# A feature map in SBUF with the batches of a chain innermost, in a kernel of row and column scans

## The chip, the cores and the metric

The kernel runs on one NeuronCore of a Trainium2 chip. The metric is the device time of one execution in microseconds (us); for several executions it is the median. The profile and the trace come from one further execution, taken by the hardware profiler. TensorE (PE) does the matrix products and reads its moving operand from SBUF; VectorE (DVE), ScalarE (ACT) and GpSimd (POOL) do the rest; SyncE (SP) issues the transfers between HBM and SBUF.

## The reference

Two layers follow each other, each `x + scan(groupnorm(x))`. The input is float32, 32 batches of 48 channels, 64 rows and 128 columns. A scan runs over the map four times, and each pass goes step by step: down over the rows, up, right over the columns, left. A step adds to a row (or column) the five-tap convolution of the one before it, taken along the row (or column), over all 48 channels:

```python
def step(w, b):
    def f(carry, inp):
        nxt = inp + _conv1d(carry, w, b)      # 48 x 48 channels, 5 taps, padding 2
        return (nxt, nxt)
    return f
...
x = x + scan0(_gn(x)); x = x + scan1(_gn(x))  # _gn: 16 groups of 3 channels
```

Down and up share their weights. The 32 batches are independent of each other; within one, each step needs the result of the step before it.

## The kernel before

**Tiling.** Channels of even positions along the convolved axis sit on partitions 0 to 47, those of odd positions on 64 to 111, so one step is three accumulated matrix products of 112 x 112 (lines 173, 174 and 177 of `step`): with the pair of positions itself, the pair before and the pair after. In float32 each product is two matmul instructions in the trace, so a step is six. The moving operand of a step has the pairs of positions of four batches: 4 x 64 columns in the down and up passes, 4 x 32 in the right and left passes; the second and third product leave out one pair at the edge (4 x 63 and 4 x 31).

**The map.** Four batches (G = 4) make a chain, and the map of a chain is one tile `[112, G, 64, 2, 32]`: batch, pair of columns, r, pair of rows. It is 64 KB on each partition. `row(h)` (line 195) is every 64th element of it, one element at a time: 256 elements, 256 bytes apart within a batch. `col(v)` (line 198) is four runs of 32 adjacent elements, one for each batch.

**The step.** After its products a VectorE instruction on line 180 adds the PSUM tile, the bias and `inp` (a row or column of the map) and writes `dst`. In the down pass `inp` and `dst` are the same row of the map, and the next step's moving operand is that row; the last row of the pass goes to the tile `last`, which is contiguous. In the up pass `dst` and the moving operand are `carry` tiles, contiguous, and `place` (line 188) copies each carry with two ScalarE instructions of 48 partitions into the map, where the right and left passes read it. In those passes `inp`, `dst` and the moving operand are columns of the map.

**Two lanes.** Two chains, one for each lane, are in flight in turn: while VectorE finishes a step of one lane, PE runs the six matmuls of the other. "Round" below means one step of both lanes, 12 matmuls. There are eight chains, so four pairs of them one after the other, each with two layers: eight times down, up, right and left.

**Boundaries.** Between two layers of a pair (and between two pairs) each batch goes through `add_scan` (line 106, POOL: adds the map of the batch to its x tile of 112 x 4096), the store, where the next chain starts the load of its x, the statistics of the group norm (lines 119 to 145, mostly VectorE) and `normalize`: two ScalarE instructions (line 152, partitions 0 to 47) and two POOL instructions (line 159, partitions 64 to 111), each of 48 x 2048, which read x with a step of 128 elements and write runs of the map. The first down step needs all four batches of its chain. The order of the instructions on each engine is set by the tile framework when the program is built; each engine runs its own in that order.

Of the kernel before, what the change touches and what calls it, by code (L numbers as in the profile page):

```python
"""Two pre-activation layers x + scan(groupnorm(x)), each scan running down, up, right and
left over the feature map with a 5-tap convolution across the other axis per step.

Layout. Channels of even and odd positions along the convolved axis sit side by side on the
partitions (even at 0..47, odd at 64..111, zeros between), so that one convolution step is
three accumulated 112 x 112 matrix products: with the pair before, the pair itself and the
pair after. The map of a batch lies in SBUF as [pair of w][r][pair of h]:
  down/up:     partition side = parity of w, r = parity of h
  right/left:  partition side = parity of h, r = parity of w
The scans run in place; the up scan writes its rows to where the second layout has them.  # L10

Batches go in chains of G, and two chains are in flight step by step in turn, so that what
a step of one chain waits for runs under the other's matrix products.
"""
# [7 lines left out]
F32 = mybir.dt.float32  # L22
# [5 lines left out]
P = ODD + C  # L28
# [11 lines left out]
def kernel(  # L40
# [34 lines left out]
        cpool.tile([P, G, WP, 2, HP], F32, tag=f"map{i}", name=f"map{i}")  # L75
# [3 lines left out]
        cpool.tile([P, G, WP], F32, tag=f"last{i}", name=f"last{i}") for i in range(LANES)  # L79
# [3 lines left out]
    # The partitions between the two sides carry zeros throughout.  # L83
# [10 lines left out]
    def load_x(lane: int, src: bass.AP, b: int) -> bass.AP:  # L94
        """Batch j of a chain always goes to tile j % NX of its lane."""
# [9 lines left out]
    def add_scan(lane: int, j: int, xt: bass.AP):  # L105
        nc.gpsimd.tensor_tensor(  # L106
            xt, xt, maps[lane][:, j].rearrange("c p r q -> c q (p r)"), ALU.add
        )

    def stats(xt: bass.AP, key: str):  # L110
        """Per-partition scale and offset of the group norm of one batch."""
# [21 lines left out]
        # 1 / sqrt(var), with a Newton step behind the table's square root.  # L133
# [14 lines left out]
    def normalize(lane: int, j: int, xt: bass.AP, scale: bass.AP, offset: bass.AP):  # L148
        view = xt.rearrange("c q (p r) -> c p r q", r=2)
        for hs in range(2):  # L150
            hsl = SIDES[hs]
            nc.scalar.activation(  # L152
                maps[lane][SIDES[0], j, :, hs, :],
# [6 lines left out]
                maps[lane][SIDES[1], j, :, hs, :],  # L160
# [7 lines left out]
    def step(lane: int, layer: int, way: int, key: str, prev, inp, dst):  # L168
        """dst = inp + conv(prev) + bias over [P, G, pairs]."""
# [20 lines left out]
    def scan(lane: int, layer: int, key: str, early):  # L190
# [3 lines left out]
        def row(h):  # L194
            return m[:, :, :, h % 2, h // 2]
# [119 lines left out]
```

## Time and profile before

| | |
|---|---|
| Median of the 3 timed runs | 8442.6 us |
| Lowest and highest | 8436.63 and 8445.32 us |
| Span of the profiled execution | 8440.7 us |
| PE busy | 6745.4 us, 80% |
| VectorE busy | 3721.4 us, 44% |
| ScalarE busy | 1902.0 us, 23% |
| GpSimd busy | 1264.6 us, 15% |
| DMA queue of the loads and stores | 20.7% of the 16 engines |

The span runs from the first to the last instruction of the profiled execution. Busy shares are means over stages that differ: in the passes PE is busy nearly throughout, at the boundaries hardly at all. [...] The timeline gives start and duration of instructions; those that follow each other with the same form are merged, with their count.

### The profile page before, as it was taken

How to read it: one execution, taken by the hardware profiler on the slowest of the kernel's cores; microseconds unless marked ns; L12 is line 12 of the kernel's file. 1: busy time of each engine (PE TensorE's matmuls, PEld its weight loads, DVE VectorE, ACT ScalarE, POOL GpSimd, SP SyncE). 2: the span in 40 equal slices, each digit the busy share in tenths (PEclk: the TensorE clock that was granted, in tenths of full speed). 3: DMA queues.
4: the chain of work that ended last, by engine and by line, in shares of the span. 5: the costliest groups of instructions: out<-in, count | busy, mean ns of one | idle time of the engine just before them, and what ended most of it. 6: DMA issues, size and time to landing. Idle time of an engine off the chain costs nothing. (4 is left out here: it accounts for less than half of the span.)

```text
span 8440.7 us, 85243 instructions
## 1 busy us (share of the span) xinstructions
PE 6745.4 (80%) x36736; PEld 5026.5 (60%) x36736; DVE 3721.4 (44%) x7235; ACT 1902.0 (23%) x2241; POOL 1264.6 (15%) x199
## 2 busy tenths in 40 slices
PE   4999559994499955999449995599944999559993
PEld 2479524894247952489424795248942479524893
DVE  5345533553334553355333455335532345533552
ACT  3070110700207011070020701107012070110700
POOL 4000330003300033000330003300043000330004
PEclk9999779997699977999769997799976999779997
DMA  9000240005700024000570002400057000340005
GB/s 94 0 1 1 44 76 0 1 1 74 105 0 1 1 41 79 0 1 1 75 105 0 1 1 46 74 0 1 1 75 105 0 1 1 46 74 0 1 1 90
DMA packets 497403, 258.09 MB, mean 31 GB/s; under 512 B 5392, under 2 KB 496912, under 8 KB 497024
## 3 DMA queue, kind: packets, MB, share of 16 engines
q1 hardware_dynamic: 496640, 251.68, 20.7%
q8 instruction: 287, 4.70, 0.2%
q10 hardware_dynamic: 384, 0.96, 0.0%
q14 instruction: 92, 0.75, 0.0%
HBM read 151.95 MB, written 100.66 MB: 30 GB/s over the span
## 5 line engine op out<-in xcount | busy, mean ns | idle before, releaser
L106 POOL TENSOR_TENSOR x<-x,map 112x4096 f32<-112x4096 f32 x64 | 694.3, 10866 | 6611.4 <-issue 3290.5
L123 PE MATMUL ps_stat_x<-mv_x,mask_sb 112*112 112x1 f32 x64 | 16.4, 326 | 728.1 <-DVE mv_x L121 722.2
L188 ACT COPY map<-last 48x256 f32<-48x256 f32 x32 | 21.9, 683 | 2469.5 <-DVE last L180 2469.2
L123 PEld LDWEIGHTS ps_stat_x<-mv_x,mask_sb 112*112 112x112 f32 x64 | 14.9, 286 | 731.8 <-DVE mv_x L121 724.8
L135 ACT ACTIVATE std_m<-var_m 112x1 f32<-112x1 f32 x32 | 6.5, 203 | 1850.4 <-DVE var_m L132 1850.3
L123 PE MATMUL ps_stat_m<-mv_m,mask_sb 112*112 112x1 f32 x64 | 16.4, 326 | 473.8 <-DVE mv_m L121 448.6
L119 DVE BATCH_NORM_STATS2 st_x<-x 112x6 f32<-112x512 f32 x256 | 155.6, 679 | 513.9 <-DMA x<-in_x 513.7
L135 ACT ACTIVATE std_x<-var_x 112x1 f32<-112x1 f32 x32 | 6.5, 203 | 1615.1 <-DVE var_x L132 1615.1
L159 POOL TENSOR_SCALAR map<-x,scale_x,offset_x 48x2048 f32<-48x2048 f32 x64 | 277.8, 4341 | 346.3 <-DVE offset_x L145 340.3
L119 DVE BATCH_NORM_STATS2 st_m<-x 112x6 f32<-112x512 f32 x256 | 160.5, 679 | 340.7 <-POOL x L106 340.7
L159 POOL TENSOR_SCALAR map<-x,scale_m,offset_m 48x2048 f32<-48x2048 f32 x64 | 271.6, 4244 | 195.4 <-DVE offset_m L145 171.3
L123 PEld LDWEIGHTS ps_stat_m<-mv_m,mask_sb 112*112 112x112 f32 x64 | 14.9, 286 | 477.7 <-DVE mv_m L121 450.7
L152 ACT ACTIVATE map<-x,offset_x,scale_x 48x2048 f32<-48x2048 f32 x64 | 279.3, 4364 | 44.9 <-DVE offset_x L145 41.3
L152 ACT ACTIVATE map<-x,offset_m,scale_m 48x2048 f32<-48x2048 f32 x64 | 273.1, 4268 | 51.6 <-DVE offset_m L145 34.1
L130 PE MATMUL ps_stat_m<-sq_m,mask_sb 112*112 112x1 f32 x64 | 16.5, 328 | 151.9 <-DVE sq_m L129 151.9
L180 DVE SCALAR_TENSOR_TENSOR map<-ps_1L1d,b_sb,map 112x256 f32<-112x256 f32 x62 | 75.3, 1215 | 123.7 <-PE ps_1L1d L177 117.9
L180 DVE SCALAR_TENSOR_TENSOR map<-ps_3L1d,b_sb,map 112x256 f32<-112x256 f32 x62 | 75.5, 1217 | 123.1 <-PE ps_3L1d L177 118.0
L180 DVE SCALAR_TENSOR_TENSOR map<-ps_7L0d,b_sb,map 112x256 f32<-112x256 f32 x62 | 76.3, 1231 | 121.2 <-PE ps_7L0d L177 115.6
L180 DVE SCALAR_TENSOR_TENSOR map<-ps_7L1d,b_sb,map 112x256 f32<-112x256 f32 x62 | 75.5, 1217 | 123.0 <-PE ps_7L1d L177 117.9
L180 DVE SCALAR_TENSOR_TENSOR map<-ps_5L1d,b_sb,map 112x256 f32<-112x256 f32 x62 | 75.4, 1216 | 123.0 <-PE ps_5L1d L177 117.9
L180 DVE SCALAR_TENSOR_TENSOR map<-ps_3L0d,b_sb,map 112x256 f32<-112x256 f32 x62 | 76.4, 1232 | 120.7 <-PE ps_3L0d L177 115.4
L180 DVE SCALAR_TENSOR_TENSOR map<-ps_5L0d,b_sb,map 112x256 f32<-112x256 f32 x62 | 76.3, 1231 | 120.6 <-PE ps_5L0d L177 115.5
(617 smaller groups left out, 19622.9 us busy)
## 6 DMA issues: line engine op xcount, KB each, us to landing
x<-in_x SPq DMA_DIRECT2D x128, 768.0 KB, 16.3
mid<-x SPq DMA_DIRECT2D x64, 768.0 KB, 12.1
x<-mid SPq DMA_DIRECT2D x64, 768.0 KB, 16.0
out<-x SPq DMA_DIRECT2D x64, 768.0 KB, 12.6
w_sb<-in_w ACTq DMA_DIRECT2D x1, 882.0 KB, 12.2
mask_sb<-in_mask ACTq DMA_DIRECT2D x1, 49.0 KB, 1.9
b_sb<-in_b ACTq DMA_DIRECT2D x1, 2.6 KB, 5.4
```

What stands on the lines that cost most here:

```text
L106: nc.gpsimd.tensor_tensor(xt, xt, maps[lane][:, j].rearrange("c p r q -> c q (p r)"), ALU.add)
L119: nc.vector.bn_stats(st[:, s, :], flat[:, bass.ts(s, SEG)])
L123: nc.tensor.matmul(ps[:, 0:1], mask_sb, mv[:, 0:1], start=True, stop=True)
L130: nc.tensor.matmul(ps[:, 1:2], mask_sb, sq, start=True, stop=True)
L135: nc.scalar.activation(std, var, AF.Sqrt)
L152: nc.scalar.activation(maps[lane][SIDES[0], j, :, hs, :], view[hsl, :, 0, :], AF.Identity, bias=offset[hsl], scale=scale[hsl],)
L159: nc.gpsimd.tensor_scalar(maps[lane][SIDES[1], j, :, hs, :], view[hsl, :, 1, :], scale[hsl], offset[hsl], ALU.mult, ALU.add,)
L180: nc.vector.scalar_tensor_tensor(dst, ps, b_sb[:, layer, way : way + 1], inp, ALU.add, ALU.add)
L188: nc.scalar.copy(maps[lane][SIDES[hs], :, :, ws, q], carry[SIDES[ws]])
```

## The change

The map, `last`, the carries and the PSUM tile of a step get the four batches as their innermost dimension. The map becomes `[112, 64, 2, 32, G]`: pair of columns, r, pair of rows, batch. `row(h)` is then 64 runs of four adjacent elements, 1024 bytes from one to the next, and `col(v)` one run of 128 adjacent elements. `place` reads a contiguous carry and writes 64 runs of four; `normalize` writes and `add_scan` reads single elements of one batch, 16 bytes from one pair of rows to the next in `normalize`, and 512 bytes from one column to the next in `add_scan`, where it was 128. The numbers of instructions, the engines, the loads, the stores and the arithmetic stay.

```diff
-        cpool.tile([P, G, WP, 2, HP], F32, tag=f"map{i}", name=f"map{i}")
+        cpool.tile([P, WP, 2, HP, G], F32, tag=f"map{i}", name=f"map{i}")
...
-        cpool.tile([P, G, WP], F32, tag=f"last{i}", name=f"last{i}") for i in range(LANES)
+        cpool.tile([P, WP, G], F32, tag=f"last{i}", name=f"last{i}") for i in range(LANES)
...
     def add_scan(lane: int, j: int, xt: bass.AP):
-            xt, xt, maps[lane][:, j].rearrange("c p r q -> c q (p r)"), ALU.add
+            xt, xt, maps[lane][:, :, :, :, j].rearrange("c p r q -> c q (p r)"), ALU.add
...
     # normalize
-                maps[lane][SIDES[0], j, :, hs, :],
+                maps[lane][SIDES[0], :, hs, :, j],
...
-                maps[lane][SIDES[1], j, :, hs, :],
+                maps[lane][SIDES[1], :, hs, :, j],
...
     # step
-        n = prev.shape[2]
-        ps = ps_scan.tile([P, G, n], F32, tag=f"ps{lane}", name=f"ps_{key}")
+        n = prev.shape[1]
+        ps = ps_scan.tile([P, n, G], F32, tag=f"ps{lane}", name=f"ps_{key}")
...
-            ps[:, :, 1:n], wt[:, 0], prev[:, :, 0 : n - 1], start=False, stop=False
+            ps[:, 1:n], wt[:, 0], prev[:, 0 : n - 1], start=False, stop=False
...
-            ps[:, :, 0 : n - 1], wt[:, 2], prev[:, :, 1:n], start=False, stop=True
+            ps[:, 0 : n - 1], wt[:, 2], prev[:, 1:n], start=False, stop=True
...
     # place
-            nc.scalar.copy(maps[lane][SIDES[hs], :, :, ws, q], carry[SIDES[ws]])
+            nc.scalar.copy(maps[lane][SIDES[hs], :, ws, q, :], carry[SIDES[ws]])
...
     # scan: row(h), col(v), carry
-            return m[:, :, :, h % 2, h // 2]
+            return m[:, :, h % 2, h // 2, :]
...
-            return m[:, :, v // 2, v % 2, :]
+            return m[:, v // 2, v % 2, :, :]
...
-                [P, G, WP], F32, tag=f"carry{lane}", name=f"carry_{key}u{h}"
+                [P, WP, G], F32, tag=f"carry{lane}", name=f"carry_{key}u{h}"
```

## Rows read from the trace of the kernel before

**Rows 1.** The page: its first line, the span and the instruction count.

```profile
span 8440.7 us, 85243 instructions
```

**Rows 2.** Windows, down stages, settled: first, last, sum of eight; columns in the head.

```profile
core 0: us, PE busy (x) PEld busy (x) DVE busy (x) ACT busy (x) POOL busy (x), PEclk, DMA share, GB/s
182.30:451.00 268.70, 268.70 (x631) 121.49 (x630) 106.09 (x105) 1.38 (x2) 0.00 (x0) 1.00 0.00 0
7527.80:7801.80 274.00, 274.00 (x643) 123.77 (x642) 107.94 (x107) 1.38 (x2) 0.00 (x0) 1.00 0.00 0
sum 2140.80, PE 2140.80 PEld 967.33 DVE 844.47 ACT 11.05 POOL 0.00; mean PE 267.60 PEld 120.92 DVE 105.56 ACT 1.38 POOL 0.00
```

**Rows 3.** Windows, the eight beginnings of the down stages: first and sum.

```profile
136.20:182.30 46.10, 45.33 (x105) 21.90 (x105) 16.08 (x17) 3.80 (x1) 3.88 (x1) 0.93 0.47 54
sum 367.90, PE 359.76 PEld 173.36 DVE 122.37 ACT 31.39 POOL 32.16; mean PE 44.97 PEld 21.67 DVE 15.30 ACT 3.92 POOL 4.02
```

**Rows 4.** Timeline of PE before both lanes run: start, duration, engine, line, count.

```profile
1138.81 1.03 PE L174 MATMUL ps_0L1d<-map,w_sb 112*112 112x252 f32 x2
1139.66 1.02 PE L177 MATMUL ps_0L1d<-map,w_sb 112*112 112x252 f32 x2
```

**Rows 5.** Timeline of one half round of an up stage, all engines.

```profile
520.95 0.59 PE L173 MATMUL ps_1L0u<-carry_1L0u,w_sb 112*112 112x256 f32 x2
521.21 0.68 DVE L180 SCALAR_TENSOR_TENSOR carry_0L0u<-ps_0L0u,b_sb,map 112x256 f32<-112x256 f32 x1 [0.52 <-PE ps_0L0u L177]
522.02 0.39 PEld L173 LDWEIGHTS ps_0L0u<-carry_0L0u,w_sb 112*112 112x112 f32 x2
522.24 0.59 PE L173 MATMUL ps_0L0u<-carry_0L0u,w_sb 112*112 112x256 f32 x2
```

**Rows 6.** Windows, the eight up stages: first and sum.

```profile
451.00:619.40 168.40, 164.87 (x755) 128.28 (x753) 87.18 (x127) 163.70 (x252) 0.00 (x0) 1.00 0.00 1
sum 1348.90, PE 1320.76 PEld 1025.45 DVE 699.33 ACT 1309.48 POOL 0.00; mean PE 165.10 PEld 128.18 DVE 87.42 ACT 163.68 POOL 0.00
```

**Rows 7.** Groups by form, VectorE, down stage of the first two chains: busy, mean ns.

```profile
L180 DVE SCALAR_TENSOR_TENSOR map<-ps_0L0d,b_sb,map 112x256 f32<-112x256 f32 x62 | 48.0, 774 | 82.3 <-PE ps_0L0d L177 72.7 <-ACT map L152 9.5
L180 DVE SCALAR_TENSOR_TENSOR map<-ps_1L0d,b_sb,map 112x256 f32<-112x256 f32 x62 | 76.3, 1231 | 120.4 <-PE ps_1L0d L177 115.4 <-POOL map L159 5.0
L180 DVE SCALAR_TENSOR_TENSOR last<-ps_0L0d,b_sb,map x1: 643/643/643, 447.8 to 447.8; 112x256 f32<-112x256 f32 x1
```

**Rows 8.** Tile view of a carry, VectorE: minimum, median, maximum ns.

```profile
L180 DVE SCALAR_TENSOR_TENSOR carry_0L0u<-ps_0L0u,b_sb,last x1: 484/484/484, 614.9 to 614.9; 112x256 f32<-112x256 f32 x1
```

**Rows 9.** Windows, the eight right and left stages: sum.

```profile
sum 2749.40, PE 2745.86 PEld 2743.67 DVE 1426.11 ACT 14.80 POOL 3.25; mean PE 343.23 PEld 342.96 DVE 178.26 ACT 1.85 POOL 0.41
```

**Rows 10.** Windows, start, boundaries and end: two boundaries and the sum of nine.

```profile
962.90:1163.00 200.10, 23.68 (x65) 15.39 (x65) 89.74 (x149) 66.55 (x24) 150.93 (x24) 0.51 0.60 98
1989.10:2249.40 260.30, 20.94 (x59) 13.80 (x59) 58.80 (x149) 68.64 (x24) 152.86 (x24) 0.51 0.98 137
sum 1833.70, PE 178.22 PEld 116.72 DVE 629.13 ACT 535.27 POOL 1229.21; mean PE 19.80 PEld 12.97 DVE 69.90 ACT 59.47 POOL 136.58
```

**Rows 11.** The page's groups of the adding and normalising instructions.

```profile
L106 POOL TENSOR_TENSOR x<-x,map 112x4096 f32<-112x4096 f32 x64 | 694.3, 10866 | 6611.4 <-issue 3290.5
L159 POOL TENSOR_SCALAR map<-x,scale_m,offset_m 48x2048 f32<-48x2048 f32 x64 | 271.6, 4244 | 195.4 <-DVE offset_m L145 171.3
L152 ACT ACTIVATE map<-x,offset_m,scale_m 48x2048 f32<-48x2048 f32 x64 | 273.1, 4268 | 51.6 <-DVE offset_m L145 34.1
```

**Rows 12.** Timeline of POOL: start, boundary between layers, boundary between chains.

```profile
78.32 8.36 POOL L159 TENSOR_SCALAR map<-x,scale_x,offset_x 48x2048 f32<-48x2048 f32 x2 [2.54 <-DVE offset_x L145]
...
1035.12 17.90 POOL L159 TENSOR_SCALAR map<-x,scale_m,offset_m 48x2048 f32<-48x2048 f32 x4 [1.98 <-DVE offset_m L145]
1100.58 8.39 POOL L159 TENSOR_SCALAR map<-x,scale_m,offset_m 48x2048 f32<-48x2048 f32 x2 [8.81 <-DVE offset_m L145]
...
2184.97 8.21 POOL L159 TENSOR_SCALAR map<-x,scale_x,offset_x 48x2048 f32<-48x2048 f32 x2 [26.57 <-DVE offset_x L145]
```

## The prediction, made before the changed kernel had run

> **What bounds the kernel now.** I read the page's span first [rows 1], then cut it into stages with the view by windows, since the page's busy shares mix stages that have different limits. The cuts are at the first matmuls of each pass. The down stages take 2140.8 us settled [rows 2] and 367.9 us in their beginnings, while the lanes come in [rows 3]; the up stages 1348.9 [rows 6]; right and left 2749.4 [rows 9]; the start, the boundaries and the end 1833.7 [rows 10]. That is the whole span of 8440.7 us.
>
> [...] The eight windows hold 5029 matmuls (631 in the first, 643 in the last), so one comes every 2140.8 / 5029 = 425.7 ns. The same number of columns in the up stage goes twice as fast: from the first matmul of one lane to the first of the other, six matmuls, it is 522.24 - 520.95 = 1.29 us, or 215 ns each, also at full clock [rows 5, 6]. Weights, columns and output are alike; what differs is that the down pass reads single elements 256 bytes apart and the up pass a contiguous carry. So half of the down stage is the price of that read. VectorE has time to spare in it: 844 of 2140.8 us [rows 2].
>
> In the up stages ScalarE is busy 1309.5 of 1348.9 us and PE 1320.8 [rows 6]: the placing copies (252 in the window, 650 ns each) and the matmuls are nearly level, ScalarE a little longer. Right and left are PE's (2745.9 of 2749.4) [rows 9]. At the boundaries PE has next to nothing to do, and POOL is busy 1229 of 1833.7 us [rows 10].
>
> **The change part by part.** *Matmuls of the down pass.* The moving operand becomes runs of four adjacent elements. The trace has no run of four: it has runs of one at 425.7 ns and long runs at 215 [rows 2, 5]; runs of 32 (right and left) make 112.8 ns for half the columns (2749.4 us / 24384 matmuls), close to the long runs [rows 9]. These are the bounds. I take 215, since a run of four already hands over four elements from adjacent addresses and only a single element shows the price. Settled stages: 5029 x (425.7 - 215) = 1060 us saved.
>
> [...]
>
> *Beginnings of the down stages.* Here the clock is granted only in part (0.93 in the first [rows 3], and 0.51 over a boundary [rows 10]). [...] Bounds: 0, and 367.9 x (1 - 215 / 425.7) = 182 us; I take 100.
>
> *VectorE on line 180.* With everything contiguous the instruction takes 484 ns [rows 8]; with a row of the map read by single elements 643, with one read and written 774 in lane 0 and 1231 in lane 1 [rows 7]. It gets shorter, between 484 and 774. That saves nothing itself: it is hidden by the other lane's matmuls. What matters is that it still fits when these take half the time. The up stage shows the room: VectorE starts at 521.21, the weights of that lane's next step are loaded at 522.02, 0.81 us later [rows 5]. Up to some 0.75 us is covered; what is over that is paid in each round.
>
> *Placing copies.* Contiguous read as before, writes in runs of four instead of one. As long as four take less than the 12 matmuls of a round (12 x 215 = 2.58 us, so under 645 ns each) PE sets the pace: 6048 matmuls x 215 ns = 1300 us against 1348.9, less what the ends of the stages keep. Bounds 0 (copies as now) and 49; I take 40. A loss I exclude: the same elements go in longer runs.
>
> *Right and left.* Four runs of 32 become one of 128. Bounds: 0, and (112.8 - 107.5) x 24384 = 129 us if all that is over half an up matmul came from the runs. I take 0: in a step half as long the change of lanes comes twice as often, which explains as much.
>
> *Adding (line 106).* POOL reads the map with steps of 512 bytes instead of 128, single elements in both. One takes 10.87 us, 2.65 ns an element of two operands; POOL's normalising instruction, which reads x with the 512-byte step, takes 4244 / 2048 = 2.07 [rows 11]. No row shows a longer step to be dearer. Bounds: 0, and 0.58 x 4096 = 2.4 us saved on each of some 58 that lie on the path (eight per layer boundary, six per chain boundary, eight at the end), 138 us. I take 0, since a second operand also explains the difference.
>
> *Normalising (lines 152, 159).* This is the cost. Writes of 2048 adjacent elements become single elements 16 bytes apart, while x is read with a step as before. No row has such a write on ScalarE or POOL; the nearest is VectorE's line 180, which reads a row by single elements and writes either contiguously (643 ns) or by single elements (774 or 1231) [rows 7]. That is 0.51 or 2.30 ns an element more, so 1.05 or 4.7 us on an instruction of 4.24 to 4.27 us now [rows 11]; the bound below is 0, if read and write overlap wholly. I take 1.05: the 1231 comes up in only one lane, while PE reads the other map, and PE hardly reads at a boundary. Both engines do their halves side by side, so one of each counts once. On the path: the whole 16 at the start (POOL idles only the 2.54 us that the statistics need after the instruction before); in a layer boundary 15 of 16, which go in chains with adding and statistics (17.9 us for four, then one pair after each addition); in a chain boundary, where loads and stores stand between them, about 10 [rows 12]. Together 16 + 4 x 15 + 3 x 10 = 106, so +111 us, with bounds 0 and 106 x 4.7 = 498.
>
> [...]
>
> No wait, transfer or instruction is added, and none is moved past another queue.
>
> Sum: 8440.7 - 1060 - 100 - 40 + 111 = 7352 us. The median of the runs is 1.9 us above the profiled span, which gives 7354; I say **7350**, 0.87 of before.
>
> **The rivals.** *Partial gain on PE.* Each run of four costs one element time more: 256 + 64 columns, 215 x 1.25 = 269 ns. Then 5029 x (425.7 - 269) = 788 us are saved and some 75 in the beginnings: 7650 us. For it: no row shows a short run. Against it: runs of 32 show almost no such price [rows 9].
>
> *VectorE becomes late.* The two lanes run the same instruction in 774 and 1231 ns [rows 7], so what another engine does at that time costs it up to 457 ns. While lane 1's instruction runs, PE reads lane 0's map at the same offset as VectorE in lane 1's; that stays so in the new layout. If one lane kept 1231 ns, it would be 0.48 us over the cover in each of about 62 rounds, eight times: 238 us, so 7590. Against it: the instruction touches 64 places of a row instead of 256, and a quarter of 457 ns on top of 484 is covered.
>
> *Normalising at the upper bound.* 4.7 us on each: 7354 - 111 + 498 = 7740 us.
>
> *No gain on PE, slower.* If the read is paid by its step from place to place, however many elements lie there, or if matmuls take these patterns one element at a time, the down matmul stays at about 425.7 ns, while normalising still pays its 111 us and placing gives 40: 8514 us. It decides as soon as a down matmul gains less than 71 / 5900 = 12 ns. Against it stands the almost full rate of runs of 32.
>
> **How the numbers follow.** The forecast has 0.75, with a range of its own of 7200 to 7500 from the bounds of normalising, adding and the right and left stages. Partial gain, late VectorE and dear normalising have 0.07 each, no gain on PE 0.04. The range of 7180 to 7660 holds nearly all of the forecast, the late VectorE and the partial gain; it leaves out dear normalising, no gain and the tails. A measurement of this kernel can tell about 0.2% from no change; all cases but the last are far on the fast side, so faster has 0.95, slower 0.04 and no change 0.01.
>
> **What would show it.** Right: matmuls of the down pass at 215 ns with PE still busy throughout, settled down stages of about 135 us each, line 180 there at 480 to 650 ns in both lanes, placing copies well under 645 ns, up stages of about 164 us, right and left as now. The price would stand in lines 152 and 159 at about 5.3 us and in layer boundaries of about 215 us. Wrong: gaps of PE before line 173 that end with VectorE's line 180 (the late VectorE), a down matmul near 270 or 425 ns, or lines 152 and 159 far above 5.3 us. A different order of POOL's additions and normalising instructions at the boundaries, which the sum leaves out, would also move it.

## The result, and the profile after

The changed kernel takes 7138.0 us (median of four runs, 7134.5 to 7142.7) against 8439.6 for the kernel before (the three runs of the table above and one more): 0.8457 of it, with a 95% interval of 0.8445 to 0.8469. The forecast was 7350. The direction and the main place of the gain were right, its size was 212 us too small, and the time lies below the stated range of 7180 to 7660. The profiled executions differ by 8440.7 - 7139.2 = 1301.5 us of span.

The page of the changed kernel, first line:

```profile
span 7139.2 us, 85243 instructions
```

The view by windows of the changed kernel (columns as in [rows 2]; PEclk is the granted clock of TensorE as a share of its full speed), cut at the same events as before: the first down stage from where it is settled, the first beginning of a down stage, the sum of the eight whole down stages, of the eight up stages and of right and left, and the sum of start, boundaries and end. In this kernel, every line number from the addition on is one higher than before.

```profile
182.30:290.00 107.70, 107.70 (x506) 89.25 (x505) 40.65 (x84) 0.00 (x0) 0.00 (x0) 1.00 0.00 1
...
135.60:182.30 46.70, 46.04 (x191) 35.94 (x192) 14.74 (x31) 3.85 (x1) 4.12 (x1) 1.00 0.51 55
...
sum 1294.50, PE 1286.64 PEld 1049.19 DVE 467.92 ACT 42.68 POOL 34.01; mean PE 160.83 PEld 131.15 DVE 58.49 ACT 5.33 POOL 4.25
...
sum 1281.90, PE 1281.90 PEld 1060.80 DVE 483.84 ACT 805.71 POOL 0.00; mean PE 160.24 PEld 132.60 DVE 60.48 ACT 100.71 POOL 0.00
...
sum 2732.60, PE 2726.15 PEld 2722.50 DVE 1429.57 ACT 8.97 POOL 3.98; mean PE 340.77 PEld 340.31 DVE 178.70 ACT 1.12 POOL 0.50
...
sum 1830.20, PE 178.86 PEld 119.35 DVE 625.60 ACT 545.06 POOL 1241.76; mean PE 19.87 PEld 13.26 DVE 69.51 ACT 60.56 POOL 137.97
```

A matmul of the settled down stage now comes every 107.70 / 506 = 212.8 ns, and PE is still busy throughout. With 5029 matmuls that is 5029 x (425.7 - 212.8) = 1071 us of the gain [rows 2]; the whole down stages went from 2140.8 + 367.9 = 2508.7 to 1294.5, so the beginnings gave the other 143 [rows 2, 3].

| Stage | Before | After | Measured | In the sum |
|---|---|---|---|---|
| Down, settled | 2140.8 | | -1071 | -1060 |
| Down, beginnings | 367.9 | | -143 | -100 |
| Up | 1348.9 | 1281.9 | -67 | -40 |
| Right and left | 2749.4 | 2732.6 | -17 | 0 |
| Start, boundaries, end | 1833.7 | 1830.2 | -4 | +111 |
| Sum | 8440.7 | 7139.2 | -1301.5 | -1089 |

The timeline of a half round of a settled down stage after (start, duration, engine, line), to be held against [rows 5]:

```profile
205.29 0.59 PE L174 MATMUL ps_0L0d<-map,w_sb 112*112 112x256 f32 x2
205.49 0.48 DVE L181 SCALAR_TENSOR_TENSOR map<-ps_1L0d,b_sb,map 112x256 f32<-112x256 f32 x1 [0.80 <-PE ps_1L0d L178]
...
206.36 0.39 PEld L174 LDWEIGHTS ps_1L0d<-map,w_sb 112*112 112x112 f32 x2
206.57 0.59 PE L174 MATMUL ps_1L0d<-map,w_sb 112*112 112x256 f32 x2
```

Six matmuls in 206.57 - 205.29 = 1.28 us: the down pass has the pitch of the up pass. VectorE ends at 205.97, 0.39 us ahead of the weights that wait for it at 206.36, so it isn't late. The groups by form show it at the contiguous price of [rows 8], and no longer at 774 and 1231 [rows 7]. The line is lane 1's; lane 0's has 483 ns:

```profile
L181 DVE SCALAR_TENSOR_TENSOR map<-ps_1L0d,b_sb,map 112x256 f32<-112x256 f32 x62 | 30.0, 484 | 60.8 <-PE ps_1L0d L178 55.1 <-POOL map L160 5.7
```

The page's groups after, for the boundaries (busy, mean ns), answer to [rows 11]: the addition as before, and normalising 0.12 to 0.15 us dearer in the layer boundaries, not 1.05. In the groups of the start and the chain boundaries (scale_x) it is 0.06 and 0.10 us.

```profile
L107 POOL TENSOR_TENSOR x<-x,map 112x4096 f32<-112x4096 f32 x64 | 693.6, 10850 | 5310.1 <-issue 2639.2
...
L160 POOL TENSOR_SCALAR map<-x,scale_m,offset_m 48x2048 f32<-48x2048 f32 x64 | 281.0, 4390 | 193.0 <-DVE offset_m L146 169.1
...
L153 ACT ACTIVATE map<-x,offset_m,scale_m 48x2048 f32<-48x2048 f32 x64 | 280.5, 4383 | 50.5 <-DVE offset_m L146 33.1
```

The placing copies, in the view of their line after (minimum, median, maximum ns), fell from 650 to 403:

```profile
L189 ACT COPY map<-carry_0L0u x126: 401/403/405, 299.6 to 459.0; 48x256 f32<-48x256 f32 x126
```

ScalarE is therefore busy 805.7 us of the up stages and PE all of 1281.9. That also changes the start of the right stage. In the kernel before, its first matmul (timeline; the bracket has the idle time before it and what ended it) and the window behind it:

```profile
619.37 0.77 PE L173 MATMUL ps_0L0r<-map,w_sb 112*112 112x128 f32 x2 [3.53 <-ACT map L188]
...
619.30:624.60 5.30, 5.23 (x25) 5.22 (x26) 1.05 (x3) 1.89 (x4) 0.00 (x0) 0.50 0.00 0
```

and the same place after:

```profile
459.00:464.50 5.50, 5.11 (x45) 4.84 (x44) 2.59 (x7) 1.20 (x3) 0.00 (x0) 1.00 0.00 0
```

Before, ScalarE was behind with its copies: PE stood idle for 3.53 us until the last ones were done, and the first 5.3 us of the right stage then ran at a granted clock of 0.50: 25 matmuls, where after it are 45 at 1.00.

### The profile page after: what moved, and what is told of

Its sections match the earlier page's. It is cut to its first block, busy times and chain, and to the rows that moved or that the text cites. A ratio compares the mean times of both kernels' runs of the same rounds, so it can differ in the third digit from the quotient of the medians.

```text
span 7139.2 us, 85243 instructions
## 1 busy us (share of the span) xinstructions
PE 5473.6 (77%) x36736; PEld 4951.8 (69%) x36736; DVE 3006.9 (42%) x7235; ACT 1402.4 (20%) x2241; POOL 1279.8 (18%) x199
## 5 line engine op out<-in xcount | busy, mean ns | idle before, releaser
L160 POOL TENSOR_SCALAR map<-x,scale_x,offset_x 48x2048 f32<-48x2048 f32 x64 | 284.4, 4443 | 333.6 <-DVE offset_x L146 327.7
L160 POOL TENSOR_SCALAR map<-x,scale_m,offset_m 48x2048 f32<-48x2048 f32 x64 | 281.0, 4390 | 193.0 <-DVE offset_m L146 169.1
L153 ACT ACTIVATE map<-x,offset_m,scale_m 48x2048 f32<-48x2048 f32 x64 | 280.5, 4383 | 50.5 <-DVE offset_m L146 33.1
L131 PEld LDWEIGHTS ps_stat_m<-sq_m,mask_sb 112*112 112x112 f32 x64 | 14.3, 285 | 157.1 <-DVE sq_m L130 157.1
L130 DVE SCALAR_TENSOR_TENSOR sq_m<-dev_m,mv_m 112x1 f32<-112x1 f32 x32 | 78.1, 2439 | 0.7
L181 DVE SCALAR_TENSOR_TENSOR map<-ps_1L0r,b_sb,map 112x128 f32<-112x128 f32 x127 | 44.6, 351 | 44.6 <-PE ps_1L0r L178 44.6
L181 DVE SCALAR_TENSOR_TENSOR map<-ps_7L0r,b_sb,map 112x128 f32<-112x128 f32 x127 | 44.6, 351 | 44.5 <-PE ps_7L0r L178 44.5
L181 DVE SCALAR_TENSOR_TENSOR map<-ps_5L0r,b_sb,map 112x128 f32<-112x128 f32 x127 | 44.6, 351 | 44.5 <-PE ps_5L0r L178 44.5
L181 DVE SCALAR_TENSOR_TENSOR map<-ps_3L0r,b_sb,map 112x128 f32<-112x128 f32 x127 | 44.6, 351 | 44.3 <-PE ps_3L0r L178 44.3
L181 DVE SCALAR_TENSOR_TENSOR map<-ps_3L1r,b_sb,map 112x128 f32<-112x128 f32 x127 | 44.6, 351 | 44.2 <-PE ps_3L1r L178 44.2
```

The lines of the kernel that those rows point to most:

```text
L130: nc.vector.scalar_tensor_tensor(sq, dev, dev, mv[:, 1:2], ALU.mult, ALU.add)
L131: nc.tensor.matmul(ps[:, 1:2], mask_sb, sq, start=True, stop=True)
L153: nc.scalar.activation(maps[lane][SIDES[0], :, hs, :, j], view[hsl, :, 0, :], AF.Identity, bias=offset[hsl], scale=scale[hsl],)
L160: nc.gpsimd.tensor_scalar(maps[lane][SIDES[1], :, hs, :, j], view[hsl, :, 1, :], scale[hsl], offset[hsl], ALU.mult, ALU.add,)
L181: nc.vector.scalar_tensor_tensor(dst, ps, b_sb[:, layer, way : way + 1], inp, ALU.add, ALU.add)
```

## The experiments

Four questions were open: what in the new pattern gives TensorE its full rate (several elements in one aligned group of 16 bytes, or simply longer runs), why the single-element write of normalising costs next to nothing, what the up and right stages gained, and what became of the 457 ns between the lanes. What the answers pointed to at the boundaries comes last.

**A list of prices.** A kernel that issues single instructions of the kernel's shapes with other patterns, eight of each (TensorE: 24 products, which are 48 matmul instructions). VectorE's part runs while the other three rest; ScalarE's and GpSimd's parts run side by side, as normalising does in the kernel, and TensorE's beside GpSimd's additions:

```python
# VectorE, 256 elements: PSUM + SBUF, steps counted in elements
nc.vector.scalar_tensor_tensor(spaced(dst, 256, 64), flat(ps, 1), bb, spaced(src, 256, 64), ...)
# ScalarE, GpSimd: 48 x 2048, read with a step of 128 or contiguous, write contiguous or 16 bytes apart
nc.scalar.activation(new_map(0), x_view(0), AF.Identity, bias=..., scale=...)
# TensorE: singles, runs of 2, 4, 8, 16; runs of 4 from the second, from the third element
nc.tensor.matmul(pm[k % 2][:, 0:252], w_sb, spaced(dst, 252, 256, 4, 1), start=True, stop=True)
```

> Leaves out the whole computation: the input is copied to the output, and single instructions are run eight or 24 times with different patterns. VectorE's addition, contiguous 484 ns. If its price in the old down pass came from the patterns alone, reading singles gives about 643 and reading and writing them in place about 774; if the other engine was part of it, 774 is not reached when TensorE is idle. A write of singles 16 bytes apart: as dear as at 256 bytes by the prediction's step (about 640 and 770), near 484 and 643 if short steps are cheap. Normalising on ScalarE and GpSimd: read by steps 4.2 us; contiguous read with a write 16 bytes apart near 2 us if the write is free, near 4 if not. The addition on GpSimd 10.85 us with steps of 128 and of 512 bytes alike. TensorE, 256 columns: contiguous and runs of 32 to 4 at 212 ns; runs of 2 at 212 if two are enough, else between 212 and 425; singles at 425; runs of four that start on the second or third element of 16 bytes slower if the line counts, the same if it does not.

TensorE first, in its timeline (start, duration, then the line; the time of 48 instructions is best read from one start to the next). The lines are: 146 contiguous, 149 runs of 16, 155 runs of four, 158 runs of two, 161 single elements, 164 runs of four from the second element, 167 from the third, 170 runs of two from the second, 173 every second element.

```profile
307.00 10.52 PE L146 MATMUL pm<-dst,w_sb 112*112 112x256 f32 x48
317.36 10.52 PE L149 MATMUL pm<-dst,w_sb 112*112 112x256 f32 x48
...
338.08 10.52 PE L155 MATMUL pm<-dst,w_sb 112*112 112x256 f32 x48
348.44 10.56 PE L158 MATMUL pm<-dst,w_sb 112*112 112x256 f32 x48
358.84 20.85 PE L161 MATMUL pm<-dst,w_sb 112*112 112x256 f32 x48
379.51 12.34 PE L164 MATMUL pm<-dst,w_sb 112*112 112x252 f32 x48
391.69 10.40 PE L167 MATMUL pm<-dst,w_sb 112*112 112x252 f32 x48
401.93 10.40 PE L170 MATMUL pm<-dst,w_sb 112*112 112x252 f32 x48
412.17 10.98 PE L173 MATMUL pm<-dst,w_sb 112*112 112x256 f32 x48
```

Contiguous, runs of four: 10.36 us, 216 ns an instruction. Runs of two: 10.40. Single elements: 20.67, or 431 ns, the pitch of the old down pass. Runs of four that start at the second element of a group of four (one aligned group of 16 bytes has three of them, the next has one): 12.18 / 48 = 254 ns, though from the third element (two and two) it is 10.24 / 48 = 213. So in these runs it is not the length of the run that counts: it is how many of its elements stand in one aligned group of four. Two or more adjacent ones in one group cost nothing extra (10.36 to 10.40 us for 256 columns, 10.24 for 252). Two with a gap between them (line 173) cost little: 10.98 us by the duration of the 48, where contiguous has 10.52. A lone one does cost: (254 - 213) / 63 = 0.64 ns each for the 63 of them in 252 columns, and (431 - 216) / 256 = 0.84 ns where all are alone, at 0.84 ns for an element itself.

Next the groups of the list (busy, mean ns). VectorE with a PSUM operand: 74 single elements read, 80 read and written, 89 written 16 bytes apart, 95 runs of four (contiguous and runs of two have the same 484). ScalarE: 98 contiguous, 101 read with a step of 128 elements, 104 written 16 bytes apart, 107 both. GpSimd: 116 contiguous, 119 the stepped read, 122 the 16-byte write, 125 both; its addition: 134 contiguous, 140 with the map in 512-byte steps.

```profile
L140 POOL TENSOR_TENSOR xt<-xt,dst 112x4096 f32<-112x4096 f32 x8 | 86.9, 10864 | 0.6
L134 POOL TENSOR_TENSOR xt<-xt,dst 112x4096 f32<-112x4096 f32 x8 | 70.6, 8831 | 0.6
...
L107 ACT ACTIVATE dst<-xt,b_sb 48x2048 f32<-48x2048 f32 x8 | 32.5, 4060 | 0.3
L125 POOL TENSOR_SCALAR dst<-xt,b_sb 48x2048 f32<-48x2048 f32 x8 | 32.2, 4026 | 0.8
L104 ACT ACTIVATE dst<-xt,b_sb 48x2048 f32<-48x2048 f32 x8 | 31.8, 3976 | 0.3
L122 POOL TENSOR_SCALAR dst<-xt,b_sb 48x2048 f32<-48x2048 f32 x8 | 31.7, 3968 | 0.8
...
L101 ACT ACTIVATE dst<-xt,b_sb 48x2048 f32<-48x2048 f32 x8 | 30.7, 3836 | 0.3
...
L119 POOL TENSOR_SCALAR dst<-xt,b_sb 48x2048 f32<-48x2048 f32 x8 | 30.3, 3788 | 0.8
...
L98 ACT ACTIVATE dst<-xt,b_sb 48x2048 f32<-48x2048 f32 x8 | 16.7, 2093 | 82.7 <-DVE dst L95 82.4
L116 POOL TENSOR_SCALAR dst<-xt,b_sb 48x2048 f32<-48x2048 f32 x8 | 16.4, 2054 | 87.3 <-DVEq L229 86.6
...
L80 DVE SCALAR_TENSOR_TENSOR dst<-ps,b_sb,src 112x256 f32<-112x256 f32 x8 | 6.1, 757 | 0.3
...
L89 DVE SCALAR_TENSOR_TENSOR dst<-ps,b_sb,src 112x256 f32<-112x256 f32 x8 | 5.3, 668 | 0.3
...
L74 DVE SCALAR_TENSOR_TENSOR dst<-ps,b_sb,src 112x256 f32<-112x256 f32 x8 | 5.1, 640 | 0.3
...
L95 DVE SCALAR_TENSOR_TENSOR dst<-ps,b_sb,dst 112x256 f32<-112x256 f32 x8 | 3.9, 484 | 0.3
```

On ScalarE a stepped read alone costs 3836 - 2093 = 1.74 us, the 16-byte write alone 1.88, and both together 1.97, not 3.62: the two overlap, and together cost little more than the dearer one. GpSimd does the same: 2.05 us contiguous, 3.97 with the write alone, and the write adds 4026 - 3788 = 0.24 us to an instruction that already has the stepped read. That is close to the prediction's lower bound ("if read and write overlap wholly"), and the row it leaned on instead, VectorE's 643 and 774, belongs to an engine where the second price comes on top in good part (640 for the read, 757 for both). GpSimd's addition takes the 10.86 us of the kernel with steps of 512 bytes; contiguous it is 8.83, so the stepped read costs 2.0 us there, before the change (10.87 [rows 11]) and after.

The number of groups that a row touches shows no price: 256 elements in runs of two lie in 128 groups of 16 bytes, a contiguous row in 64, and they take the same within 0.4% (10.40 and 10.36 us for the 48).

**Runs of two in the kernel.** Two batches innermost, two outermost:

```diff
-        cpool.tile([P, WP, 2, HP, G], F32, ...)
+        cpool.tile([P, 2, WP, 2, HP, 2], F32, ...)
```

> The changed kernel with runs of two: two batches innermost and the other two outermost. If two adjacent elements are enough for a full-rate read, the down matmul stays at 212 ns and the time at 7120 to 7170 us. Rival, each run costs something: with one element more for each run, 212 x 1.5 = 318 ns, 6048 down matmuls, 640 us more, about 7780 us; with no gain at all below four, 425 ns and about 8430 us.

7136.9 us, 0.846 of before (0.8446 to 0.8474): the same as runs of four. Its window and VectorE's group in the down stage of lane 1 (lane 0's has 639 ns):

```profile
182.30:290.00 107.70, 107.70 (x504) 86.95 (x503) 57.54 (x84) 0.00 (x0) 0.00 (x0) 1.00 0.00 1
```

```profile
L181 DVE SCALAR_TENSOR_TENSOR map<-ps_1L0d,b_sb,map 112x256 f32<-112x256 f32 x62 | 43.4, 700 | 50.4 <-PE ps_1L0d L178 43.6 <-ACT map L153 6.9
```

504 matmuls in the 107.70 us that held 506 with runs of four: TensorE does not tell two from four. VectorE does here: 639 and 700 ns against 484 for runs of four, and 484 for runs of two in the list with TensorE at rest. But it stays below the 0.75 us that the prediction found covered, and the time does not move.

**The map one element later.** The change with the map's first element 4 bytes further on, so that each run of four has three elements in one aligned group of 16 bytes and one in the next; run length, steps and instructions stay:

```diff
+        cpool.tile([P, WP * 2 * HP * G + 4], F32, ...)
...
+        t[:, 1 : 1 + WP * 2 * HP * G].rearrange("c (p r q g) -> c p r q g", p=WP, r=2, q=HP)
```

> The changed kernel with both maps one element (4 bytes) later, so that each run of four has three elements in one 16-byte line and one in the next. If a line of 16 bytes with one element in it costs an element's time, as the price list has it (252 columns in 253.8 ns from the second element, 213.3 from the third), the down matmul goes from 214 to 254 ns: 6048 x 0.041 = 250 us more, 7360 to 7420 us. Rival, only the length of the run counts: 7120 to 7160 us.

7372.7 us, 0.8744 of before (0.8728 to 0.8759), 235 us more than with the map aligned. The same window of the down stage:

```profile
182.30:290.00 107.70, 107.70 (x425) 75.21 (x424) 36.16 (x71) 0.00 (x0) 0.00 (x0) 1.00 0.00 0
```

107.70 / 425 = 253 ns, the list's 254. Over the 6048 matmuls of the down stages it is 6048 x (253.4 - 212.8) = 246 us. The run length alone is refuted as the cause, and something near the prediction's rival of a partial gain (269 ns) is what one gets when the map is not aligned.

**Normalising, two runs.** First the layout that normalising and adding use is put back, on the new map:

```diff
+        flat = maps[lane].rearrange("c p r q g -> c (p r q g)")
+        return flat.rearrange("c (g p r q) -> c g p r q", g=G, p=WP, r=2)
...
-                maps[lane][SIDES[0], :, hs, :, j],
+                old_view(lane)[SIDES[0], j, :, hs, :],
```

> The changed kernel, with only the boundary undone: normalising writes, and the addition reads, the places that the old layout had (runs of 32 for normalising, steps of 128 bytes for the addition); the scans keep the new layout, so the map gets its values at wrong places. Theory now: on ScalarE and GpSimd the single-element write goes on beside the stepped read and costs next to nothing, about 0.13 us an instruction on 106 instructions of the path, 14 us: 7105 to 7145 us, lines of normalising back at 4.24 to 4.34 us. Rival, the prediction's own price: 1.05 us an instruction is really paid, and something else at the boundaries gave it back: 7030 to 7090 us.

6866.1 us, 0.8139 of before (0.8126 to 0.8151): 272 us less than the change, a miss for both expectations. Its timeline of GpSimd shows why; the scans of that layer end just ahead of 798.8:

```profile
756.13 21.83 POOL L111 TENSOR_TENSOR x<-x,map 112x4096 f32<-112x4096 f32 x2 [614.07 <-issue]
798.84 21.66 POOL L111 TENSOR_TENSOR x<-x,map 112x4096 f32<-112x4096 f32 x2 [20.88 <-DVE map L185]
```

With the old places, the addition of a batch covers one quarter of the columns of the scan, and two of the four additions run 42 us early, under the left scan. So the run doesn't price the write by its time. Its groups of normalising have 4255 to 4339 ns against 4383 to 4443, some 0.1 us, and the early additions pointed to the boundaries, below.

Second, normalising reads x in runs of 32 and writes as the change does:

```diff
-        view = xt.rearrange("c q (p r) -> c p r q", r=2)
+        view = xt.rearrange("c q w -> c (q w)").rearrange("c (r p q) -> c p r q", r=2, p=WP)
```

> The changed kernel, with normalising reading x in runs of 32 in place of steps of 512 bytes; it writes single elements 16 bytes apart as in the changed kernel. The values of x come in a wrong order. Theory one, read and write each have a price and the dearer one sets the pace: the instruction stays near 3.6 to 4.4 us and the time within 7138 plus or minus 40 us. Theory two, the write at 16 bytes costs nothing and the read alone sets the pace: the instruction falls to about 2 us, and 106 of them on the path give some 240 us, so about 6900 us.

7083.6 us in one execution, 54 less than the change. The groups of ScalarE and GpSimd:

```profile
L153 ACT ACTIVATE map<-x,offset_m,scale_m 48x2048 f32<-48x2048 f32 x64 | 255.9, 3999 | 50.5 <-DVE offset_m L146 33.0 <-DVE dev_m L128 8.3 <-DMA x<-in_x 8.3
...
L160 POOL TENSOR_SCALAR map<-x,scale_m,offset_m 48x2048 f32<-48x2048 f32 x64 | 253.2, 3957 | 191.6 <-DVE offset_m L146 168.3 <-DVE dev_m L128 20.0
```

Taking the stepped read away saves 0.38 us of 4.38 on ScalarE and 0.43 of 4.39 on GpSimd: the 16-byte write alone holds the instruction at nearly the same time. On the 106 instructions of the path that is 40 to 46 us, somewhat less than the 54.

**The up stage of the kernel before.** Its second placing copy goes to GpSimd, which is idle in the up stage; everything else as before:

```diff
-            nc.scalar.copy(maps[lane][SIDES[hs], :, :, ws, q], carry[SIDES[ws]])
+            to = maps[lane][SIDES[hs], :, :, ws, q]
+            if ws:
+                nc.gpsimd.tensor_copy(to, carry[SIDES[ws]])
+            else:
+                nc.scalar.copy(to, carry[SIDES[ws]])
```

> The kernel before, with the second of the two placing copies on GpSimd, which is idle in the scans; nothing else. If ScalarE's copies set the pace of the old up stage and delayed the right stage behind it, the up stage goes from 168.6 to 160 to 163 us and the right stage no longer starts at the low clock: 50 to 85 us less, 8355 to 8390 us. Rival, the up stage is TensorE's own: within 10 us of the kernel before.

8362.5 us, 0.9915 of before (0.99 to 0.9931), 69 us less and within its first expectation. Window of the start of its first right stage:

```profile
612.40:618.00 5.60, 5.17 (x44) 4.83 (x44) 2.59 (x7) 0.63 (x2) 0.64 (x2) 1.00 0.00 0
```

The copies there still take 620 to 630 ns each, but one for each engine. The 3.53 us of idle time at the start of the right stage are gone (PE is idle for 0.43 us of this window), and with them the fall of the clock (1.00 here). Up, right and left gained 67 + 17 = 84 us together in the change; the split copies give 69 of them, and their first up stage is 162.0 us long against 160.3 after, which over eight stages is the other 14. So their gain was ScalarE's copies, in the rounds and at the end, and not the longer runs that TensorE reads in right and left.

**The 457 ns between the lanes.** The kernel before, with the map of lane 1 shifted 64 bytes:

```diff
+        cpool.tile([P, G * WP * 2 * HP + 16 * i], F32, ...)
...
+        t[:, 16 * i :].rearrange("c (g p r q) -> c g p r q", g=G, p=WP, r=2)
```

> The kernel before, with the map of lane 1 later by 64 bytes. If VectorE's 1231 ns in lane 1 comes from TensorE reading the other map at the same offset within 256 bytes, it falls to 760 to 800 ns, as in lane 0. Rival, the reason is another one (order of the lanes, PSUM): 774 and 1231 stay. The time stays within 20 us of the kernel before by either, since VectorE is covered in the old down stage.

8424.5 us in one execution, beside a median of 8431.0 for the kernel before. VectorE in lane 1's down stage:

```profile
L184 DVE SCALAR_TENSOR_TENSOR map<-ps_1L0d,b_sb,map 112x256 f32<-112x256 f32 x62 | 47.1, 759 | 120.6 <-PE ps_1L0d L181 120.6
```

From 1231 [rows 7] to 759, which is the list's 757 with TensorE at rest. The 457 ns came from where the two maps lie relative to each other while TensorE reads the one and VectorE works in the other, as the late-VectorE rival had it; how the chip comes to it isn't shown. It was hidden in the kernel before, and in the new layout it doesn't arise (484 ns in both lanes). The 639 and 700 ns of the runs of two may be the same thing; no run separates that.

**The boundaries.** The early additions can be had on the layout of the change: the first two batches of a chain are loaded earlier, and GpSimd adds their columns 32 to 127 while the left scan works on columns 31 to 0.

```diff
+    def add_scan(lane: int, j: int, xt: bass.AP, w0: int = 0, w1: int = W):
+        part = xt[:, :, w0:w1]
+        scanned = maps[lane][:, w0 // 2 : w1 // 2, :, :, j]
...
-            if v == 24:
+            if v == 56:
                 early()
+            if v == CUT - 2:
+                partly()
```

> The changed kernel; the first two batches of each lane are loaded at column 56 of the left scan in place of 24, and GpSimd adds their columns 32 to 127 once the left scan has passed them; only columns 0 to 31 are left for the boundary. Theory from the run with the boundary in the old places, whose two early additions went under the scan: four additions of 10.85 us stand in a row behind each scan, three quarters of that can go under it, 32 us at each of eight scans, so 6870 to 6920 us. Rival, what is saved is waited for elsewhere (loads, statistics) or GpSimd's reads slow VectorE's steps: above 7060 us.

6966.0 us, 0.8258 of before (0.8245 to 0.8271): 172 us less than the change. That is less than the 256 of the first expectation, and between its range and the rival's. VectorE's steps are not slowed: they take 351 ns each beside GpSimd's additions and without them. GpSimd at a layer boundary and at a chain boundary:

```profile
797.01 11.28 POOL L111 TENSOR_TENSOR x<-x,map 112x1024 f32<-112x1024 f32 x4 [9.88 <-DVE map L185]
...
961.75 8.55 POOL L164 TENSOR_SCALAR map<-x,scale_m,offset_m 48x2048 f32<-48x2048 f32 x2 [9.92 <-DVE offset_m L150]
...
1867.54 9.64 POOL L164 TENSOR_SCALAR map<-x,scale_x,offset_x 48x2048 f32<-48x2048 f32 x2 [10.57 <-DVE offset_x L150]
```

After the scan the additions take 11.3 us instead of 43.3, and a layer boundary, from the scan's end to the last normalising, 970.3 - 797.0 = 173.3 us instead of 205.5. That is the 32 us. A chain boundary gets only some 9 us shorter (1867.5 + 9.6 - 1627.9 = 249.3 us, 258.2 in the change), because there the transfers are busy nearly throughout (a DMA share of 0.96 to 0.98 in the windows of these boundaries after the change). In the first of them VectorE's statistics wait 153.5 us for loads of x, and 162.9 in the change. 4 x 32 + 3 x 9 = 155, and the end, 14 us shorter, has most of the rest.

The same question for the additions that remain: on VectorE instead of GpSimd, in the changed kernel and on top of the early additions.

```diff
-        nc.gpsimd.tensor_tensor(
+        nc.vector.tensor_tensor(
```

> The kernel after, with the additions of the boundaries on VectorE instead of GpSimd. What it tests: what the unchanged 10.85 us additions cost on the path, which the sum left alone. VectorE has not been timed on this form; from its single-instruction prices (484 ns for 256 elements contiguous, 640 with single elements read) 4096 elements with a stepped read come to an estimated 6.8 us. If GpSimd's row of addition, then normalising, sets the layer boundaries: the four additions at the end of a scan shrink from 43.3 to about 27 us, and in the second half of a layer boundary the period of a batch falls from 28.1 us (8.5 normalising, 10.85 adding, 8.8 statistics) to about 16, since VectorE adds and takes statistics while GpSimd normalises: some 65 us less in each of four layer boundaries, little in the chain boundaries, where loads and stores are busy throughout: 6800 to 6900 us. If loads and stores set the layer boundaries as well (they are busy for about 120 of 200 us there), no more than 80 us is to be had in each and any shortfall shows as idle time of VectorE that a transfer ends: 6900 to 7050 us.

> The kernel with two additions of each chain made early under the left scan (GpSimd, columns 32 to 127), and the rest of the additions at the boundaries on VectorE instead of GpSimd. The early additions alone gave 172 us: 32 us in each of four layer boundaries and about 9 in each chain boundary. If the remaining gain is GpSimd's row of addition and normalising, the layer boundaries get another 40 us shorter (periods of a batch of 28.1 us become about 16): 6770 to 6830 us. If the transfers are the next bound in the layer boundaries, it comes out within 40 us of the version with all additions on VectorE, and the idle time of VectorE there ends with a load.

All additions on VectorE: 6964.8 us, 0.8252 of before (0.824 to 0.8264). Early additions and the rest on VectorE: 6838.6 us, 0.81 (0.8086 to 0.8113), the fastest here, 0.958 of the change (6838.6 / 7138.0). Both come out above the times of their first expectations. The first time lies in the range of its second expectation, but not by that mechanism: in the first layer boundary VectorE waits for no transfer. With all additions on VectorE that boundary took 163.1 us (797.25 to 960.39 in its timeline), 42 less than in the change where 65 were expected; 4 x 42 = 168 is nearly all of the 173 us gained. With the early additions on top it took 142.0, 31 less than with the early additions alone, where 40 were expected, and the time is 126 us below that of the first version, so transfers are not the next bound there. The timeline of the first one says what was missing: while VectorE adds, GpSimd's normalising takes longer.

```profile
925.90 7.40 DVE L107 TENSOR_TENSOR x<-x,map 112x4096 f32<-112x4096 f32 x1
926.02 4.23 ACT L153 ACTIVATE map<-x,offset_m,scale_m 48x2048 f32<-48x2048 f32 x1 [1.13 <-DVE offset_m L146]
926.14 10.99 POOL L160 TENSOR_SCALAR map<-x,scale_m,offset_m 48x2048 f32<-48x2048 f32 x1 [2.48 <-DMA mid<-x]
```

And the group of the second one in the layer boundaries, where it was 4390 ns in the change:

```profile
L165 POOL TENSOR_SCALAR map<-x,scale_m,offset_m 48x2048 f32<-48x2048 f32 x64 | 386.9, 6046 | 221.4 <-DVE offset_m L151 218.3
```

In the chain boundaries of the same run, where the additions and normalising do not meet, it is 4352 ns. VectorE's addition takes 7.4 us (6.8 were estimated). The same normalising instruction that takes ScalarE 4.23 us beside it takes GpSimd 10.99: 6.6 us more than the 4.39 of the change, and 7.16 us of the addition were left when it started. How the two hold each other up is not shown. The period of a batch in the second half of a layer boundary becomes 17.6 us, not 16.

## Where the prediction was right, and why it was 212 us off

The main mechanism came true: the down pass reads at the pitch of the up pass. The time still fell below the range, because every term erred to the same side: 115 us at the boundaries, 43 in the beginnings, 27 in the up stages, 17 in right and left, 11 in the settled down stages. The range itself was drawn too tight. Its lower end is 170 us below the forecast, while the prediction's own bounds for normalising (111), the beginnings (82) and placing (9) alone allow 202.

*Matmuls of the down pass: right.* 1060 forecast, 1071 measured. The reason given ("only a single element shows the price") was nearly the right one. It lacked the alignment, which the runs showed: with the map 4 bytes later the matmul takes 253 ns. The prediction did not work out how its four floats lie in such groups; so far it was lucky.

*Beginnings of the down stages: the term was mis-sized.* The step from "the clock is granted only in part" led to 100 of the possible 182, and no run shows the 100. What the traces show is that nothing is saved at the lower clock: two down matmuls took 0.85 us before [rows 4] and 0.84 us after (from 1002.45 to 1003.29 us of its timeline), both at a granted clock of 0.50, and 0.42 us after at 1.00 (from 1006.90 to 1007.32). But the row the step rests on has 0.93 [rows 3]; 0.51 belongs to the boundary ahead of it [rows 10]. The lowest of the eight beginnings has 0.80 (the clock is the third number from the end):

```profile
6463.10:6493.50 30.40, 29.29 (x66) 14.71 (x67) 9.87 (x11) 4.17 (x1) 4.22 (x1) 0.80 0.51 67
```

Where the clock is steady it is 0.50 or 1.00 (0.50 from 168.20 to 170.20 us of the first beginning, 1.00 from 174.20 to 176.20). With these two levels the eight clocks, 0.80 to 0.93, mean that about three quarters of the beginnings ran at the full one (an estimate), and there the halving counts: 191 matmuls now where 105 fitted, in 46.7 and 46.1 us. Three quarters of 182 is 137; measured 143. The mechanism held, and the size had not been worked out from the rows.

*VectorE, covered: right.* 484 ns, within the forecast. The rival's cause was real, as the shifted lane showed, but it did not come up in the new layout.

*Placing copies: right in kind, size and bound wrong.* 40 of at most 49 were forecast, 67 came. The bound was worked out with 6048 matmuls of 215 ns; the windows hold about 752 matmuls each at 160.30 / 753 = 213 ns. And nothing was kept by the ends of the stages, for which 9 were held back. The wait at the end of the stages is 28 of the 67: PE was idle for 1348.9 - 1320.8 us of the up stages before, and is never idle in them now. "ScalarE a little longer" [rows 6] was the row that said PE waits for it there.

*Right and left: "I take 0" was off by 17.* Not the runs, which the prediction argued about, but a neighbour: the wait for the last copies (3.53 us in the first), with the lower clock behind it (0.50 for 5.3 us). The split copies in the kernel before gave most of the same gain without touching a run: the first right and left took 342.1 us with them, 343.5 before and 341.5 after.

*Adding: right at 0.* 10.87 and 10.85 us. The reason was only half of it: the second operand is not all, since a contiguous addition takes 8.83; but 128 and 512 bytes cost nearly the same.

*Normalising: the largest miss, 111 us forecast, and the boundaries came out 4 us shorter.* The step that failed is "I take 1.05", from VectorE's step from 643 to 774. On ScalarE and GpSimd a stepped read had already been paid, and the write's price overlaps with it: 0.22 and 0.24 us on top of the read in the list. In the kernels 0.06 to 0.15 us are seen, and even that isn't clearly the write's, since the unchanged instructions of the kernel before took 4244 to 4364 ns, and 4320 to 4450 in the same kernel with the shifted lane. 106 x 0.13 = 14 us would be at most what the path got. The layer boundaries show some of it: from 200.1 us [rows 10] the first one went to 200.9, and the four together from 798.2 to 803.6.

```profile
800.60:1001.50 200.90, 23.79 (x65) 15.76 (x65) 88.77 (x150) 67.77 (x24) 152.31 (x23) 0.51 0.61 98
```

That is 1.4 us for each where 15.75 (15 x 1.05) were forecast. The chain boundaries hide the rest: they went from 771.6 to 760.4 us together, with a spread among themselves of 253.5 to 260.3 before and 251.9 to 255.1 after. Why they got shorter is not shown. VectorE, from whose step the 1.05 came, took 668 ns in the list for a write with a step of four elements alone, 0.72 ns an element more than contiguous.

What stays open: why the contiguous read of x gave 54 and not 40 to 46 us, with one execution behind it; why the chain boundaries got 11 us shorter; and what in the chip makes VectorE slower when the two maps stand at the same offset.

## What to carry to other kernels

Look at TensorE's strided float32 operand by aligned groups of 16 bytes: in the runs here the stride was free where each group held a run of at least two elements (216 to 217 ns for 256 columns) and doubled the time where it held one (431). So make the innermost pair something that one instruction uses together, and align it. Price a new stride against the one that the instruction already has, not against a contiguous one, and on the engine that runs it. When a stage gets its time from two engines that are nearly level, look at the stage behind it too: here the lower clock that followed the lag (0.50 for 5.3 us) was paid there. And when several terms have their bounds on the same side, add those up before drawing the range.

## What the runs showed of the hardware beyond what was expected

- TensorE, 256 float32 columns: 216 to 217 ns in runs of two, four, 16 or contiguous, 431 as single elements; 252 columns in runs of four, where one in four stands alone in its group of 16 bytes, 254, and 213 where they are split two and two.
- 48 x 2048 elements contiguous, with a strided read, with a write 16 bytes apart, with both: ScalarE 2.09, 3.84, 3.98 and 4.06 us, GpSimd 2.05, 3.79, 3.97 and 4.03; read and write overlap. On VectorE 256 elements take 484 ns contiguous, 640 with the read and 757 with both: there they mostly add.
- VectorE's in-place row took 1231 ns beside TensorE's read at the same offset of another tile, and 759 when that tile was 64 bytes further on.
- An idle TensorE of 3.5 us was followed by 5.3 us at a granted clock of 0.50; after one of 0.39 us at the same place it stayed at 1.00.
- Beside VectorE's addition of 7.40 us, GpSimd's normalising took 10.99 us, where the change has 4.39, and ScalarE's 4.23, where it has 4.38.
